# Local attention layers: the output matmuls moved behind the scores, and the turning of queries moved behind the outputs

## The chip, the core and the metric

The kernel runs on one core of one Trainium2 chip, in one launch. The metric is the device time of an execution in microseconds (us); lower is better. The core has five engines that work side by side: PE (TensorE, matrix multiply), DVE (VectorE), ACT (ScalarE), POOL (GpSimd) and SP (SyncE, which only issues DMAs here).

## The reference, cut to what matters

Four batches of 1024 tokens with 128 features pass through two blocks. Block 0 is a linear attention and a routed mixture of experts. Block 1 is a windowed attention with a global prefix, followed by a small network of two *local layers*. The change lies in these local layers alone. One local layer computes, per batch:

```python
h = shift_token(x)                       # half of the features come from the token before
q, k, v = split(h @ wqkv, 3)             # 8 heads of 64
q, k = l2norm(q) * qs, l2norm(k) * ksc   # per head
q, k = rotary_xpos(q, k)
o = local_attention(q, k, v)             # 64-token windows, each sees itself and the one before
x = x + o @ wo
x = x + gated_mlp(layernorm(shift_token(x)))
```

Everything is computed in fp32.

## The kernel before

The local layers are done in 64 tiles of 128 tokens (2 layers x 4 batches x 8 tiles), numbered g = 0 to 63. A tile passes through a software pipeline. One pass of the main loop (L1140 ff., "iteration g") does a different step for each of several tiles:

- `scores` (L949) of tile g: 16 matmuls q·k in 64x64 pieces of the PE array (each fp32 matmul is two PE instructions, so the profile counts 32), then on DVE eight reductions (L968, tile `pr<-s`) which also give the row maximum `mx`.
- `project_mid` / `project` (L652) of tile g+3, once for queries (w=0) and once for keys (w=1): a 128x512 matmul `qk` (L658), its square on ACT (`sq`, L661), two products with the rotary tables on DVE (`co`, L663, and `si`, L668), a sum over the squares on DVE (`ss`, L670), and on POOL the sum co+si (L678) and the norm's power (L674). ACT and DVE read the same PSUM tile `qk`; in the built program the DVE instruction `co` carries a wait on ACT, for `sq`.
- `flip` (L997) of tile g-2, for each half: four PE transposes of the probabilities (`ptr`, L1002), and a copy to SBUF on ACT (`pt`, L1004).
- `over_sums` (L983) of tile g-1: division by the row sums, one half on POOL and one on DVE (L995); for a few early tiles ("light" ones) on ACT (L993).
- `exps` (L974) of tile g: eight exponentials on ACT (`pr<-pr,mx`, L980), each of which needs its reduction of `scores`.
- `turn` (L887) with w=0 of tile g+2: four PE transposes of the finished query rows `co` (`qktr`, L894), and a copy on ACT (`qT`, L901). Keys are turned by DVE and by DMA instead (`turn_keys`, L915; tiles `tk`, `kd`, `kT`).
- `outputs` (L1007) of tile g-3: 32 PE instructions with 64 columns each (`o`, L1016), then a copy on ACT (`os`, L1020).
- `values` (L934) of tile g-1: a 128x512 matmul `v` (L938) and a copy on ACT (`vs`, L940).
- side work, a few steps per iteration: `project_out` (`yp`, L1027), and the MLP of an earlier half batch: `mlp_in` (`in_m`, L1048, bn_stats on DVE), `mlp_out` (`out_m`, L160; `hn`, L161), `mlp_gate` (`gm`, L1062; three Gelu on ACT, `ge`, L1066, with a table load before them and one back to the exponential behind them), `mlp_up` (`a`, L1071; DVE, L1073), `mlp_down` (`ym`, L1079; DVE, L1080).

With half batches of four tiles, the side work repeats every four iterations: one with `mlp_gate`, one with `mlp_up` and `mlp_in`, one with `mlp_down`, one with `mlp_out` and `project_out`. In what follows these are called the gate, the up, the down and the out iteration.

PE's instructions run in the order in which the Python program writes them (`manual_schedule` for PE). The instructions of ACT, DVE, POOL and SP are put in order by a scheduler at build time, which goes by the program order and by its own estimate of when operands are ready; once built, each engine executes its list strictly in that order. Six PSUM tiles of one bank each (pool `p8m`, tag `mid`) are shared in turn by all steps but `scores`, which has two banks of its own.

Of the kernel before, what the change touches and what calls it, by code (L numbers as in the profile page):

```python
# [28 lines left out]
NT = N // P  # L29
# [19 lines left out]
def adaln_blocks(ctx: ExitStack, tc: tile.TileContext, a: dict, out: bass.AP):  # L49
# [637 lines left out]
    EARLY = 3  # L687
# [3 lines left out]
    with (  # L691
# [95 lines left out]
        def project_out(b, k):  # L787
            s = slice(k * BLK, (k + 1) * BLK)
            yp = ps.tile([P, BLK], F32, tag="m", name=f"y1_{b}_{k}")
            pe.matmul(yp, lhsT=wout1, rhs=kept1[b, k, "os"], start=True, stop=True)  # L790
            dve.scalar_tensor_tensor(xT[b][:, s], yp, mods[1][:, 2, b : b + 1], xT[b][:, s], ALU.mult, ALU.add)
# [23 lines left out]
        def when(g, f, *args):  # L815
            if 0 <= g < NG8:
                f(*divmod(g, NT), *args)
# [59 lines left out]
    with (  # L877
# [226 lines left out]
        for l in range(DEPTH):  # L1104
            for b in range(B):
                g = (l * B + b) * NT
# [33 lines left out]
        for g in range(-1, tiles + 4):  # L1140
            side = steps.get(g, [])
            when(g, scores)
            when(g + 3, project_mid, 0)

            turns = {-1: (0, 1), 0: (2,)}.get(g, (g + 2,))
            if 0 < g < NT - 2:
                when(g + 2, turn, 0)
            when(g - 2, flip, 0)
            when(g - 1, over_sums)
            when(g + 3, project_mid, 1)  # L1150
            when(g - 2, flip, 1)
            when(g, exps)
            for i in turns:
                if not 0 < g < NT - 2:
                    when(i, turn, 0)
                if i < EARLY and g < EARLY:
                    when(i, turn, 1)
            when(g - 3, outputs)
            if g > 0:
                when(g + 2, turn_keys)  # L1160
            for f, args in side[:1]:
                f(*args)

            for i in {0: (), 1: (0,)}.get(g, (g - 1,)):
                when(i, values)

            f0 = g - 7
            if f0 % 4 == 0 and 0 <= f0 < tiles - NT:
                lo = f0 % NT * P
                project_out(f0 // (B * NT), f0 // NT % B, lo, lo + BLK)  # L1170
            for f, args in side[1:]:
                f(*args)
# [127 lines left out]
```

## Time and profile before

| | |
|---|---|
| median of 3 runs | 1219.28 us (1216.90 to 1220.04) |
| the profiled execution: its time | 1217.85 us |
| its span in the profile | 1216.0 us, so 1.85 us lie around the span |
| PE busy | 1117.8 us (92%) |
| DVE busy | 893.6 us (73%) |
| ACT busy | 799.8 us (66%) |
| POOL busy | 797.0 us (66%) |
| local layers | from about 573 us to the end |
| busy shares from 840 to 940 us | PE 98.7%, DVE 93.8%, POOL 90.7%, ACT 81.0% |

The busy time of an engine is the time in which the profiler shows an instruction on it. PE's ends are modelled, so that a PE that always has an instruction is not the same as a PE that can't go faster. The chain of waits is the chain of work that ended last, followed back from the last instruction: it tells which engine the end really waited for. A line of the timeline gives the start, the length, the engine, the line of the kernel, the operation and how many were merged; "idle before" is the engine's gap ahead of it, with what ended that gap.

### The profile page before, as it was taken

Reading aid. Unit: us, or ns where it says so; the run is one execution under the profiler, and the core shown is the slowest. Engines: PE = TensorE matmul, PEld = TensorE weight load, DVE = VectorE, ACT = ScalarE, POOL = GpSimd, SP = SyncE. Lnnn points to the kernel's source line nnn. Section 1 sums busy time; section 2 is a strip of 40 time slices with the busy share of each in tenths; the row PEclk is TensorE's granted clock in tenths of the full one; section 3 lists DMA queues with packets and bytes.
Section 4 is the critical chain, followed back from the end, with each engine's and each line's share of the span. In section 5 each row is a group of like instructions: output and inputs, shape, how many; then the busy total and the mean of one; then the engine's idle time right before and its main releaser. Section 6 shows DMA issues by size and latency. Waiting matters only on the chain.

```text
span 1216.0 us, 33934 instructions
## 1 busy us (share of the span) xinstructions
PE 1117.8 (92%) x13142; PEld 677.8 (56%) x13142; DVE 893.6 (73%) x2702; ACT 799.8 (66%) x2189; POOL 797.0 (66%) x712
## 2 busy tenths in 40 slices
PE   6789998999888999978899999999999999999998
PEld 5544453444366666655665555555655556555564
DVE  5557273442475577756989999999999999999854
ACT  3353372232476677755798877878878888788772
POOL 4536454747422062516899999899998999888821
PEclk9799999999999899989999999999999999999999
DMA  6030403022132132210234333343333333333320
GB/s 183 1 125 17 140 1 119 23 66 75 28 91 74 53 101 73 68 44 23 75 114 115 100 101 92 88 111 112 106 93 87 106 109 105 110 94 99 104 59 26
DMA packets 111700, 100.68 MB, mean 83 GB/s; under 512 B 9482, under 2 KB 84788, under 8 KB 111540
## 3 DMA queue, kind: packets, MB, share of 16 engines
q1 hardware_dynamic: 111108, 98.00, 27.9%
q8 instruction: 103, 1.69, 0.6%
q10 hardware_dynamic: 432, 0.53, 0.1%
q14 instruction: 57, 0.47, 0.1%
HBM read 57.71 MB, written 20.86 MB: 65 GB/s over the span
## 4 chain that ended last, share of the span: by engine, by line
PE 43%; DVE 26%; ACT 16%; issue 6%; POOL 6%; DMA 2%; SPq 2%; POOLq 0%; ACTq 0%
PE h L496 5%; DVE pr L968 4%; ACT pr L980 4%; PE ptr L751 3%; PE qk L658 3%; DVE si L668 3%; DVE ss L670 3%; DVE tk L921 2%; DVE co L663 2%; PE yp L1027 2%; PE s L958 2%; PE s L269 2%; PE obank L768 2%; PE y L510 2%; PE gm L1062 2%
## 5 line engine op out<-in xcount | busy, mean ns | idle before, releaser
L980 ACT ACTIVATE pr<-pr,mx 128x128 f32<-128x128 f32 x512 | 200.5, 403 | 51.2 <-DVE mx L968 50.5
L678 POOL TENSOR_TENSOR co<-co,si 128x512 f32<-128x512 f32 x123 | 157.7, 1285 | 68.7 <-DVE si L668 67.4
L674 POOL TENSOR_TENSOR ss<-ss,nhalf 128x16 f32<-128x16 f32 x64 | 194.6, 3041 | 5.2
L968 DVE CUSTOM_DVE_ANT_0 pr<-s,masks,ss 128x128 f32<-128x128 f32 x512 | 144.2, 345 | 12.9 <-PE s L958 12.9
L658 PE MATMUL qk<-wqkv,hs 128*128 128x512 f32 x256 | 140.4, 631 | 4.5 <-ACT pt L753 4.5
L500 POOL TENSOR_TENSOR u<-u,cw 128x512 f32<-128x512 f32 x64 | 82.0, 1283 | 81.7 <-ACT u L498 81.7
L496 PE MATMUL h<-hT,w 128*128 128x512 f32 x256 | 122.9, 603 | 6.0 <-DVE g L502 6.0
L502 DVE TENSOR_TENSOR g<-u,h 128x512 f32<-128x512 f32 x64 | 43.9, 686 | 109.1 <-POOL u L500 109.1
L498 ACT ACTIVATE u<-h 128x512 f32<-128x512 f32 x64 | 38.2, 597 | 123.2 <-PE h L496 113.9
L663 DVE TENSOR_TENSOR co<-qk,ab 128x512 f32<-128x512 f32 x128 | 86.6, 676 | 36.1 <-ACT sq L661 36.1
L290 DVE TENSOR_REDUCE mx<-s 128x8 f32<-128x896 f32 x64 | 66.8, 1086 | 51.8 <-PE s L279 51.8
L661 ACT ACTIVATE sq<-qk 128x512 f32<-128x512 f32 x128 | 75.3, 588 | 44.4 <-PE qk L658 44.1
L980 ACT ACTIVATION_READ_ACCUMULATOR pr<-pr,mx 128x1 f32 x512 | 102.1, 199 | 0.0
L1002 PEld LDWEIGHTS ptr<-ident,pr 128*128 128x128 f32 x512 | 63.4, 141 | 63.4 <-issue 50.9
L995 POOL TENSOR_TENSOR pr<-pr,sm 128x512 f32<-128x512 f32 x64 | 78.7, 1229 | 14.2 <-DVE sm L988 7.9
L668 DVE TENSOR_TENSOR si<-qk,ab 128x512 f32<-128x512 f32 x128 | 87.1, 681 | 0.0
L496 PEld LDWEIGHTS h<-hT,w 128*128 128x128 f32 x256 | 47.7, 193 | 69.9 <-issue 50.5
L670 DVE TENSOR_REDUCE ss<-sq 128x8 f32<-128x512 f32 x128 | 86.4, 675 | 0.0
L958 PEld LDWEIGHTS s<-kT,qT 64*64 64x64 f32 x2048 | 56.4, 134 | 43.6 <-issue 24.3
L958 PE MATMUL s<-kT,qT 64*64 64x128 f32 x2048 | 72.3, 278 | 7.1 <-DMA kT<-kd 6.4
L1002 PE MATMUL ptr<-ident,pr 128*128 128x128 f32 x512 | 76.4, 273 | 0.8 <-POOL pr L995 0.7
L753 ACT COPY pt<-ptr 112x512 f32<-112x512 f32 x128 | 71.6, 612 | 8.1 <-PE ptr L751 8.0
(217 smaller groups left out, 2747.9 us busy)
## 6 DMA issues: line engine op xcount, KB each, us to landing
kT<-kd SPq DMA_DIRECT2D x53, 384.0 KB, 3.5
cw<-cd SPq DMA_DIRECT2D x128, 128.0 KB, 3.0
kd<-tk SPq DMA_DIRECT2D x61, 256.0 KB, 2.4
ve<-vs SPq DMA_DIRECT2D x120, 128.0 KB, 2.3
vb<-dv SPq DMA_DIRECT2D x32, 216.0 KB, 2.8
hs<-hT SPq DMA_DIRECT2D x16, 256.0 KB, 3.8
dv<-vt SPq DMA_DIRECT2D x32, 72.0 KB, 1.6
kT<-kd SPq DMA_DIRECT2D x8, 256.0 KB, 2.7
```

The source lines that it names most:

```text
L496: pe.matmul(hh[:, i], lhsT=w[:, c * P : (c + 1) * P], rhs=hT[b][:, blk(k)], start=True, stop=True)
L500: pool.tensor_tensor(u, u, kept[b, k, "cw"][:, c, :], ALU.mult)
L658: pe.matmul(ps, lhsT=hs[l, b][:, t * P : (t + 1) * P], rhs=wl[l][0][:, w, :], start=True, stop=True)
L663: dve.tensor_tensor(co, ph, abs_[l][:, 0, t, w, :].unsqueeze(1).to_broadcast([P, HEADS, DH]), ALU.mult)
L668: dve.tensor_tensor(si.rearrange("p h (i e) -> p h i e", i=2), ex, sn, ALU.mult)
L670: late["summed"] = dve.tensor_reduce(ss[:, w, :], sq, AX.X, ALU.add)
L674: pool.tensor_tensor(ss, ss, nhalf[:, 0:2].unsqueeze(2).to_broadcast([P, 2, HEADS]), ALU.pow)
L678: pool.tensor_tensor(co, co, si, ALU.add)
L958: pe.matmul(S[j][qs, c, :].rearrange("p (g i) -> p g i", i=32), lhsT=q[rw, c, qs], rhs=k[rw, 2 * e : 2 * e + 4, c, :], start=True, stop=True,)
L968: dve.tensor_tensor_reduce(out=pr[:, c, :], in0=S[j][:, c, :], in1=mk[:, min(t, 1), :], scale=kept[l, b, t, "ss"][:, 0, h : h + 1], scalar ...
L980: act.activation(pr[:, c, :], pr[:, c, :], AF.Exp, bias=mx[:, j, c : c + 1], scale=-1.0, accum_out=sm[:, j, c : c + 1])
L1002: pe.transpose(tp[:, c, :], pr[:, c, :], ident)
```

## The change

In each iteration `outputs` of tile g-3 moves from behind `exps` and the query turns to directly behind `scores` of tile g. `turn(g+2, w=0)` moves to directly behind `outputs`, ahead of the query projection of tile g+3. Before, it stood there or near there only for 0 < g < 6 (behind the query projection), and behind the exponentials of tile g otherwise. For g = -1 and g = 0, which fill the pipeline, the turns of tiles 0, 1 and 2 stay where they were. No instruction is added or removed: each engine has the same operations before and after, in another order.

```diff
             when(g, scores)
+            when(g - 3, outputs)
+            if g > 0:
+                when(g + 2, turn, 0)
             when(g + 3, project_mid, 0)
-
-            turns = {-1: (0, 1), 0: (2,)}.get(g, (g + 2,))
-            if 0 < g < NT - 2:
-                when(g + 2, turn, 0)
             when(g - 2, flip, 0)
             when(g - 1, over_sums)
             when(g + 3, project_mid, 1)
             when(g - 2, flip, 1)
             when(g, exps)
-            for i in turns:
-                if not 0 < g < NT - 2:
-                    when(i, turn, 0)
-                if i < EARLY and g < EARLY:
-                    when(i, turn, 1)
-            when(g - 3, outputs)
+            for i in {-1: (0, 1), 0: (2,)}.get(g, ()):
+                when(i, turn, 0)
+                when(i, turn, 1)
             if g > 0:
                 when(g + 2, turn_keys)
```

## Prediction

> **What bounds the kernel now.** I read the page first. PE is busy 92% of the span and 98.7% between 840 and 940 us, so PE looks like the bound, and the change is about PE's order. But the page's chain of waits gives PE less than half:
>
> ```profile
> PE 43%; DVE 26%; ACT 16%; issue 6%; POOL 6%; DMA 2%; SPq 2%; POOLq 0%; ACTq 0%
> ```
>
> So I asked for the chain of waits between 860 and 910 us alone, the middle of the local layers (start, length, engine, tile, line):
>
> ```profile
> 867.41 0.60 DVE hT L1028
> 868.37 0.88 ACT pr L980 x4
> ...
> 871.55 1.92 ACT pr L980 x10
> 873.48 0.47 ACT qT L901
> 873.95 0.48 ACT os L1020
> ...
> 879.36 0.49 ACT pr L980 x2
> 879.85 0.49 ACT sq L661
> 880.37 0.69 DVE co L663
> ...
> 905.68 0.59 DVE hT L1028
> 906.67 0.88 ACT pr L980 x4
> ```
>
> There is no PE piece in it. The end waits for a loop of two engines that closes once in four iterations: ACT from the first exponential of the gate iteration (868.37) to the first square of the up iteration (880.33), then DVE without a gap through the down and out iterations to the next gate iteration's first reduction (906.22), then ACT again at 906.67. The period is 906.67 - 868.37 = 38.3 us, and the scores of the gate iterations (866.72, 905.06 in the timeline) follow at the same pace. The waits from 828 to 1020 us, five periods, say the same (waiter <- releaser: total, times, longest):
>
> ```profile
> DVE co L663 <- ACT sq L661: 6.2, 5, 1.3
> DVE pr L968 <- PE s L958: 5.9, 5, 1.3
> PE in_m L1048 <- ACT qT L901: 1.2, 5, 0.3
> ```
>
> Once per period DVE stands 1.24 us for the square of the up iteration, and once 1.2 us for its scores; these are DVE's only idle stretches above 0.06 us. PE itself stands 0.3 to 0.4 us per period, for ACT's late query copy. PE is nearly full, but a faster PE alone moves neither end of the loop.
>
> **What PE saves.** PE's timeline of an out iteration (start, length; the difference of two starts is what a group costs):
>
> ```profile
> 857.53 1.12 PE L658 MATMUL qk<-wqkv,hs 128*128 128x512 f32 x2
> 858.50 0.60 PE L1002 MATMUL ptr<-ident,pr 128*128 128x128 f32 x4
> 858.93 1.02 PE L658 MATMUL qk<-wqkv,hs 128*128 128x512 f32 x2
> 859.79 0.60 PE L1002 MATMUL ptr<-ident,pr 128*128 128x128 f32 x4
> 860.23 0.60 PE L894 MATMUL qktr<-ident,co 128*128 128x128 f32 x4
> 860.76 0.34 PE L1016 MATMUL o<-pt,ve 128*64 128x64 f32 x4
> ```
>
> The projection behind the 64x64 scores takes 0.97 us to the next start, the other 0.86: 0.11 for leaving the small tiles. Four transposes cost 0.44, but 0.53 ahead of the 64-column outputs: 0.09 for entering them. Leaving the outputs costs 0.10 more ahead of the next start (0.22 against 0.12 inside the group), and 0.10 inside a 512-wide successor or 0.06 inside transposes. With scores and outputs adjacent, one full-array stretch between them goes, with one entry and one exit. Left are scores to outputs, priced like scores to projection, and outputs to query turn (0.10 + 0.06). Saved: 0.11 + 0.09 + 0.20 - 0.16 = 0.24 us, 0.20 where transposes follow; over the 61 tiles that have both steps about 61 x 0.23 = 14 us of PE time. By the Trainium skill (TensorEngine Tiling (Array Packing), "Tiling Modes") each change of tiling mode drains the array; it names no time, and scores and outputs are two modes, so by it their border is not free either, as I took it. If PE were the bound, rule and rows together would make the sum 14 us faster; by the chain they give nothing in the steady stage.
>
> **What ACT pays.** The built order of the changed program tells it. The two copies `os` and `qT` stood behind the eight exponentials; now they stand where their matmuls end, ahead of the squares. In the gate iteration ACT did two exponentials, square, copy, exponential, square, copy, five exponentials, qT, os, table load, three Gelu, vs, table load. Now: two exponentials, os, qT, exponential, square, copy, exponential, square, copy, four exponentials, table load and so on. The same instructions lie between its first exponential and the first one of the up iteration: 879.36 - 868.37 = 11.0 us both times, if nothing comes late. Nothing should: `os` can start 2.2 us after the scores begin and `qT` 2.8, ACT reaches them at 2.4 and 2.9; the first projection ends at 3.6, and ACT reaches the square at 3.7. These margins of 0.1 us are thin.
>
> In the up iteration, table load, exponential, square becomes table load, exponential, os, qT, square. Both copies are now between the loop's start and the square: 0.48 + 0.47 = 0.95 us later. DVE's `co` can't be drawn ahead of it: it waits on ACT and started at 880.37, 0.04 us behind the square's end. The Trainium skill (PSUM — Partial Sum Buffer, "PSUM bank collisions raise a hardware error") says why such a wait stands: two engines must not read one bank and quadrant at once. It speaks against this change; by it the 0.95 us are due, and without such a wait the steady stage would cost nothing.
>
> DVE also waits in the gate iteration now. Its eight reductions end 1.8 us after ACT's first exponential, the square ends at 0.8 (two exponentials) + 0.95 + 0.39 + 0.57 = 2.7: 0.9 us idle. That is covered by the 1.06 us that DVE stood before the up iteration's scores (875.79) and the 1.26 before its `co`; without that cover it would be 0.9 us more per period. In the down and out iterations os and qT come ahead of the first exponential and fill time in which ACT stood idle (2.22 us from 885.90, 1.95 us from 895.53): no cost, and DVE's stretch from 880.37 to 906.22 stays 25.85 us.
>
> So a period is 38.3 + 0.95 = 39.25 us. Twelve such periods lie between the gate iterations at 671 and 1138 us: **+11.4 us**. Bounds: 0.5 per period (6 us) if DVE makes up a part, 0.95 + 0.9 (22 us) if the second wait is not covered.
>
> **The early tiles.** In iterations 3 to 5 (593 to 620 us) ACT's new order puts the first square behind five exponentials, os and qT, for 4 and 5 behind one or two light divisions as well. From the first reduction: 0.45 + 5 x 0.39 + 0.95 + 0.39 + 0.57 = 4.3 us, while the reductions take 2.2; in iteration 5 DVE stood 0.36 us at that place. That is 1.2 to 2.0 us in each, 3.6 to 6.0; DVE's idle of 0.88, 0.35 and 1.10 us between 608 and 619 us takes some back, and iteration 6 adds under 1. I take **+4 us**, between -1 (PE is on the chain at 593 and 627 to 637 us and saves 0.2 a tile) and +8.
>
> **The rest costs nothing.** The turn now needs POOL's sum of co and si earlier: in the out iteration it ended at 855.44, and the turn starts 2.1 us behind the scores at 856.50, so 3.2 us remain; in the gate iteration 5. The outputs need `pt` copies that end 5 us before. The moved steps issue no DMA; SP's list swaps one `ve` with a `kT`, which is read over 10 us later. The six PSUM tiles rotate in another order: `in_m` now takes the bank of the key projection, about 0.3 us late, PE time off the path. The tail from 1147 us saves 0.2 us for three tiles: 0.
>
> Sum: 1217.85 + 11.4 + 4 = 1233.3 us against the profiled execution; the median was 1.4 us above that one, so I forecast **1234 us**. A measurement can tell about 0.3% (3.7 us) from no change.
>
> **Rivals.** *PE is the bound after all* (faster). For it: 98.7% busy. Then each tile is 0.23 us shorter, 1217.85 - 14 = 1204 us. Against it: no PE piece in the chain, and DVE's 25.85 us stretch has no gap to give. It decides if DVE's wait for the up iteration's square stays at 1.2 us.
> *The copies hide* (no change). ACT is 19% idle; if the 0.95 us were taken from idle time, only the early tiles would count: 1222 us. Against it: ACT's timeline has no gap from 868.37 to 885.9.
> *The second wait adds* (slower still). If DVE's 0.9 us in the gate iteration is not covered, or the thin margins are missed so that os or qT stall ACT, 12 x 0.9 = 11 us more: 1245 us.
>
> **How the numbers follow.** Forecast 0.75, with its own range 1223 to 1242 (6 to 15 steady, -1 to 8 early). PE bound 0.10, hidden 0.05, second wait 0.10. Faster 0.10, same 0.05, slower 0.85. The range 1219 to 1245 leaves out the first rival and about half of the last.
>
> **What would show it.** Right: the distance of the gate iterations' first exponentials grows from 38.3 to about 39.2; DVE's wait on ACT's square in the up iteration grows from 1.24 to about 2.3 and one of 0.9 appears in the gate iteration; scores to outputs costs PE about 0.2 between starts and the projection is 0.86; PE stands idle for other engines, over 1.5 us per period. Wrong: an unchanged or shorter period, PE in the chain of 860 to 910 us, or turns that wait for POOL.

## The result, and the profile after

The changed kernel takes 1231.6 us (median of 4 runs, 1230.19 to 1235.49), against 1218.09 us for the kernel before, measured beside it. The ratio is 1.0125 with a 95% interval of 1.0089 to 1.0161: slower by 13.5 us. The forecast was 1234 us, in a range of 1219 to 1245. The profiled execution took 1230.19 us. One of the ten runs of `up_square_first` below took 1294.72 us at a granted clock of 0.84, where all other runs quoted here had 0.97 to 0.98, and is left out.

The page of the changed kernel first: the span, PE's busy time with its share of the span and its instructions, and the engines' shares in the chain of waits.

```profile
span 1226.6 us, 33918 instructions
PE 1115.1 (91%) x13142; PEld 674.5 (55%) x13142; DVE 892.8 (73%) x2702; ACT 805.2 (66%) x2189; POOL 788.2 (64%) x712
...
DVE 37%; PE 34%; ACT 16%; issue 5%; POOL 4%; DMA 2%; SPq 1%; ACTq 0%; POOLq 0%
```

PE has less to do than before (1115.1 us against 1117.8) and its share in the chain went down, from 43% to 34%; DVE's went up, from 26% to 37%. That points to something other than PE at the end. The chain of waits between 870 and 925 us shows one full period of the loop (start, length, engine, tile, line):

```profile
870.41 0.88 ACT pr L980 x4
871.76 0.49 ACT qT L901
872.63 0.49 ACT sq L661
...
881.41 0.49 ACT pr L980 x2
882.38 0.49 ACT qT L901
882.87 0.51 ACT sq L661
883.40 0.69 DVE co L663
...
908.69 0.60 DVE pr L995
909.66 0.88 ACT pr L980 x4
```

The period is 909.66 - 870.41 = 39.25 us, where it was 38.3. In the up iteration the query copy `qT` (and the output copy `os`; the view shows the longest pieces alone) now stands between the exponential and the square, and DVE's `co` follows the square. DVE's timeline gives the two waits (in brackets: idle before, and who ended it), the first in the gate and the second in the up iteration of the changed kernel:

```profile
873.15 0.69 DVE L663 TENSOR_TENSOR co<-qk,ab 128x512 f32<-128x512 f32 x1 [0.94 <-ACT sq L661]
883.40 0.69 DVE L663 TENSOR_TENSOR co<-qk,ab 128x512 f32<-128x512 f32 x1 [2.55 <-ACT sq L661]
```

Before there was no wait for a square in the gate iteration, and 1.26 us in the up iteration:

```profile
880.37 0.69 DVE L663 TENSOR_TENSOR co<-qk,ab 128x512 f32<-128x512 f32 x1 [1.26 <-ACT sq L661]
```

The waits from 838 to 1034 us, five periods, show who now waits for ACT's copies (waiter <- releaser: total, times, longest):

```profile
DVE co L663 <- ACT sq L661: 17.4, 10, 2.6
PE a L1071 <- ACT os L1020: 5.2, 5, 1.0
```

DVE's wait was 6.2 us in five periods and is 17.4. PE stands about 1 us per period ahead of `a`, for an `os` copy that frees its PSUM tile. From 840 to 940 us PE is busy 95.8%, where it was 98.7%: 1.6 us idle per period.

To say where the 10.6 us between the two spans (1216.0 and 1226.6) lie, I cut each trace at three instructions of DVE's timeline: the first score reduction of tile 0, of tile 12 (a gate iteration) and of tile 60 (the last gate iteration). The stretches between them are called early, steady (twelve periods) and tail in what follows. A period runs from one gate iteration's first score reduction to the next one's; the fourth to the eighth of the twelve are called the middle periods (38.30 to 38.40 us before, 39.23 to 39.27 after, 38.33 and 39.24 on the mean).

| us | until tile 0 | early | steady | tail |
|---|---|---|---|---|
| before | 574.6 | 97.97 | 466.55 | 76.92 |
| after | 571.5 | 101.16 | 475.55 | 78.41 |
| difference | -3.1 | +3.2 | +9.0 | +1.5 |

The first column is code that the change doesn't touch: until 560 us each engine does the same instructions in the same order in both kernels. In the runs below it lies between 572.4 and 575.6 us with no relation to what was edited, so I count its -3.1 us as no effect of the change. The local layers lost 13.7 us.

### The profile page after: what moved, and what is told of

Read it like the earlier page. It is cut to its first block, busy times and chain, and to the rows that moved or that the text cites. A ratio compares the mean times of both kernels' runs of the same rounds, so it can differ in the third digit from the quotient of the medians.

```text
span 1226.6 us, 33918 instructions
## 1 busy us (share of the span) xinstructions
PE 1115.1 (91%) x13142; PEld 674.5 (55%) x13142; DVE 892.8 (73%) x2702; ACT 805.2 (66%) x2189; POOL 788.2 (64%) x712
## 4 chain that ended last, share of the span: by engine, by line
DVE 37%; PE 34%; ACT 16%; issue 5%; POOL 4%; DMA 2%; SPq 1%; ACTq 0%; POOLq 0%
PE h L496 6%; DVE pr L968 5%; DVE ss L670 5%; DVE si L668 4%; DVE tk L921 4%; DVE co L663 4%; PE ptr L751 3%; ACT pr L980 3%; DVE pr L995 3%; PE y L510 2%; PE s L269 2%; ACT sq L661 2%; POOL u L500 2%; PE obank L768 2%; DVE ge L1073 2%
## 5 line engine op out<-in xcount | busy, mean ns | idle before, releaser
L674 POOL TENSOR_TENSOR ss<-ss,nhalf 128x16 f32<-128x16 f32 x64 | 187.1, 2924 | 5.2
L658 PE MATMUL qk<-wqkv,hs 128*128 128x512 f32 x256 | 132.3, 600 | 5.2 <-ACT pt L753 3.7
L995 POOL TENSOR_TENSOR pr<-pr,sm 128x512 f32<-128x512 f32 x64 | 78.2, 1222 | 7.1 <-DVE sm L988 7.1
```

Source lines behind the costliest of these rows:

```text
L658: pe.matmul(ps, lhsT=hs[l, b][:, t * P : (t + 1) * P], rhs=wl[l][0][:, w, :], start=True, stop=True)
L674: pool.tensor_tensor(ss, ss, nhalf[:, 0:2].unsqueeze(2).to_broadcast([P, 2, HEADS]), ALU.pow)
L995: eng.tensor_tensor(pr, pr, bc(sm[:, j, :], [P, 4, P]), ALU.mult)
```

## The experiments

My theory: the loop of ACT and DVE bounds the steady stretch, the two copies ahead of the up iteration's square lengthen it by their 0.95 us, and PE's saving is real but off the path. The first rival: PE bounds the stretch, and the change slows PE in some way that I did not see, for example by waits on PSUM tiles in their new order. The second: the loss comes from the new order as a whole, not from that one place.

**The two copies alone, in the up and in the down iteration.** Both kernels are the kernel before with two added ACT copies of 512 columns that nobody reads, once per period of the steady stretch. Nothing else moves.

```diff
             when(g, scores)
+            if 11 < g < tiles - 3 and g % 4 == 1:      # two_copies_down: == 2
+                with tc.issue_after(kept["vs"].ins):
+                    dm = wp.tile([P, BLK], F32, tag="dm", name=f"dm_{g}", bufs=1)
+                    for i in range(2):
+                        late["dm"] = act.copy(dm, wl[0][0][:, i, :])
...
+            if w == 0 and late.get("dm") is not None:
+                order.enter_context(tc.issue_after(late.pop("dm").ins))
             act.activation(sq, ph, AF.Square)
```

> The kernel before, with two added ACT copies of a 128x512 tile (weights into a scratch tile that nobody reads) ahead of the first square of each up iteration (g = 13, 17, ... 57, twelve of them). PE's order is that of before. If the loop ACT - DVE carries the end (my theory), the square ends 0.95 us later and each later period goes from 38.3 to about 39.2 us: +9 to +12 us in all, about what the change costs, without any move on PE. If PE is the bound, ACT (19% idle in the stage) swallows them: within 2 us of before.

> The kernel before, with the same two added ACT copies, but ahead of the first square of the down iterations (g = 14, 18, ... 58), where ACT stands about 2.2 us idle. My theory: the copies fill that idle time, the period stays 38.3 us, within 2 us of before. If more ACT work costs wherever it stands: as much as in the up iterations, +9 to +12 us.

In the up iteration the copies cost 1234.84 us, ratio 1.0132 (1.009 to 1.0174): the whole loss of the change, with PE's order untouched. The steady stretch is 478.89 us (+12.3), its middle periods 39.35 to 39.40, where they were 38.30 to 38.40. Its waits from 828 to 1025 us:

```profile
DVE co L666 <- ACT sq L664: 11.4, 5, 2.3
```

2.3 us per period instead of 1.26: the copies go into DVE's wait one for one. The same two copies in the down iteration cost nothing: 1217.94 us, ratio 0.9989 (0.9965 to 1.0013), steady stretch 466.54 us. ACT's timeline there shows why:

```profile
885.35 1.30 ACT L1150 COPY dm<-wqkv 128x512 f32<-128x512 f32 x2
887.64 0.60 ACT L664 ACTIVATE sq<-qk 128x512 f32<-128x512 f32 x1 [0.99 <-PE qk L658]
```

Behind the copies ACT still stands 0.99 us for PE. So here the place decides, not the number of instructions: 1 us of ACT work costs 1.0 us per period in one iteration, and nothing in the next.

**Half of the output projection left out.** The same question from PE's side. The kernel is the one before, but only two of the four chunks of `os` are multiplied into each output projection, so that half of its contraction is missing.

```diff
-            for c in range(4):
-                pe.matmul(yp, ..., start=(c == 0), stop=(c == 3))
+            for c in range(2):
+                pe.matmul(yp, ..., start=(c == 0), stop=(c == 1))
```

> The kernel before with two of the four matmuls of each output projection left out in the local layers (half of its contraction; 4 of 8 tiles a group, some 27 us of TensorE in all). Two rivals for what bounded the kernel before. TensorE (98.7 per cent busy in the profile): the time falls by 20 to 27 us, to 1191 to 1198. The loop of ScalarE and VectorE, with TensorE only just behind it: the period of 38.3 us stays within 0.3, and the time falls by 0 to 6 us, 1212 to 1218.

PE's and DVE's timelines of one period:

```profile
861.31 1.88 PE L1027 MATMUL yp<-os,wo 128*128 128x512 f32 x4
...
878.51 0.69 DVE L663 TENSOR_TENSOR co<-qk,ab 128x512 f32<-128x512 f32 x1 [2.58 <-ACT sq L661]
```

The projection has four PE instructions instead of eight, and the scores behind it start 1.81 us later (861.31 to 863.12) where eight take 3.43 us in the changed kernel's chain of waits (at 705.89 us): about 1.6 us less PE time in every period. The middle periods stay at 38.30 to 38.37. DVE gets its scores earlier and waits all the longer for the square: 2.58 us at one place instead of 1.06 + 1.26 at two. That excludes PE as the bound of these periods. The time fell to 1211.81 us, ratio 0.9933 (0.991 to 0.9956), just below the lower end that I had given for this theory (1212). The gain of 6.2 us in the span lies in the tail (-2.8), in three of the twelve periods (the second, the ninth and the eleventh, -0.7 each) and in the early tiles (-0.9). In the tail PE counts: the chain of waits of the kernel before goes through three `yp` there. The three periods can't be put down to PE's time alone, since DVE's list was built otherwise too: in the ninth and the eleventh it has one division (L995) less ahead of the next gate iteration's first reduction.

**Each half of the change alone.** `outputs_only` moves the outputs behind the scores and leaves the turn of queries; `turn_only` moves the turn ahead of the query projection and leaves the outputs.

```diff
 outputs_only
             when(g, scores)
+            when(g - 3, outputs)
...
-            when(g - 3, outputs)
 turn_only
             when(g, scores)
-            when(g + 3, project_mid, 0)
...
-            if 0 < g < NT - 2:
+            if g > 0:
                 when(g + 2, turn, 0)
+            when(g + 3, project_mid, 0)
...                                          # and no turn behind the exponentials for g > 0
```

> Only the outputs are moved behind the scores; the turn of queries stays where it was before. ACT then does os alone ahead of the up iteration's square (table load, exponential, os, square). My theory: half of the 0.95 us per period, 0.48, so 5 to 6 us in the steady stage and 1 to 2 in the early tiles: 1222 to 1226 us. If PE is what counts, this part has nearly the whole gain on PE (scores and outputs are adjacent): faster than before, 1206 to 1210 us.

> Only the turn of queries is moved, directly behind the scores; the outputs stay where they were before. ACT then does qT alone ahead of the up iteration's square. My theory: 0.47 us per period, 5 to 6 us in the steady stage and 1 to 2 in the early tiles: 1222 to 1226 us, and both halves add up to the whole. If PE is what counts: no change, since scores and outputs are as far apart as before.

They take 1225.01 us, ratio 1.004 (1.0012 to 1.0067), and 1223.31 us, ratio 1.0027 (1.0003 to 1.0051). The middle periods are 38.85 and 38.81 us on the mean, where they were 38.33. Each half brings one ACT copy ahead of the square, and they cost 0.52 and 0.48 us per period, about one copy (0.47 to 0.48 us). ACT's way from the gate iteration's first exponential (of tile 32) to the up iteration's `co` says the same: 12.00 us before, 12.49 with either half, 12.99 with both. So no part of the loss needs the two together.

**The change, with the up iteration's copies behind the square.** For tiles 13 to 57 `os` and `qT` are copied behind the first square in the up iteration; PE's order is that of the change.

```diff
+            up = 11 < g < tiles - 3 and g % 4 == 1
+            if not up:
+                copy_out()                    # os and qT, collected by outputs and turn
             when(g + 3, project_mid, 0)
+            if up:
+                copy_out(late["sq", 0])       # issued behind the square
```

> The changed kernel with one difference: in the up iterations from g = 13 on ACT does table load, exponential, square, os, qT instead of table load, exponential, os, qT, square (the remaining exponentials follow). PE's order is that of the changed kernel. My theory: the loop gets its 0.95 us back, the period falls from 39.25 to about 38.3 us, 9 to 10 us faster than the changed kernel, so 1221 to 1223 us; what remains against before is the early tiles (about 3 us). If PE's order itself costs the time (banks, waits behind the turn), nothing changes: about 1231 us.

> The same kernel as up_square_first, for a profile at full clock: the first timing gave 1.0055 of before. My theory: a steady period of about 38.3 us, with what remains of the loss in the early tiles (about 3 us) and in the last stretch behind the gate iteration of tile 60 (about 2 us). If the steady period is well above 38.3 us, another wait has taken the place of the one removed.

The time is 1224.92 us (median of nine runs), ratio 1.0055 (1.0033 to 1.0076); the profile is of another execution of the same kernel, 1224.56 us. So half of the loss came back, less than I had expected. The middle periods are 38.53 to 38.56, not 38.3: 0.69 of the 0.91 us came back. ACT's way to the first `co` is 12.01 us again, as before. What is left lies behind it: `os` and `qT` now stand ahead of the up iteration's second square, and DVE's second `co` starts 1.95 us behind the first (883.17 to 885.12), 0.03 us behind the end of that square, where it was 1.79 (880.37 to 882.16). DVE's wait in the gate iteration is still 0.94 us; it lies within ACT's way and adds nothing to it. The rest of the loss lies where this edit does not reach, in the early tiles (100.88) and the tail (79.49).

**The squares ahead of everything.** If that square bounds the loop, it can be made earlier than it was before the change. In the up iteration ACT had: three Gelu, `vs`, table load, one exponential, square. `squares_only` has PE's order of the kernel before and only this ACT order turned, in the up iterations 13 to 57: Gelu, square, `vs`, `pt`, second square, `pt`, `qT`, `os`, table load, eight exponentials. The squares and copies need no table load, so the load moves behind them. `squares_ahead` has the same idea (the copies `os` and `qT` between the squares) with PE's order of the change for tiles 8 to 60.

```diff
 squares_only
+            up = 12 < g < tiles - 3 and g % 4 == 1
             when(g + 3, project_mid, 0)
+            if up:
+                for f in late_values:                      # the vs copy
+                    with tc.issue_after(late["sq", 0].ins):
+                        f()
...
-            when(g, exps)
+            if not up:
+                when(g, exps)
             ...
                 when(g - 3, outputs)
+                copy_out()
+                if up:
+                    when(g, exps)
 squares_ahead, against squares_only
-            early = 64 <= g < 0          # with early: outputs and turn directly behind scores
+            early = 8 <= g < 61
...
+                copy_out(late["sq", 0])
```

> The changed order on PE for g = 8 to 60, the order of before for the first eight and the last iterations; and in the up iterations ACT does the first square directly behind the Gelus, then vs, os and qT, the second square, and only then the table load and all eight exponentials. My theory: the way from the gate iteration's first exponential to the up iteration's square loses a table load (1.28), an exponential (0.39) and vs (0.58), the loop could close in about 37 us, and now PE's own time, 0.9 us per period less than before, sets the period: 37.4 to 37.8 us. That is 0.5 to 0.9 us for each of twelve periods, 6 to 10 us faster than before, 1208 to 1212 us. If the loop does not explain the loss, the time stays near 1231 or, if only the early tiles mattered, near 1219 us.

> The kernel before with its PE order unchanged, and only ACT's order in the up iterations turned: Gelus, first square, vs, copy, second square, copy, qT, os, then table load and eight exponentials. It takes the loop ACT - DVE away as the bound without the change. My theory: PE becomes the bound with the order of before, 38.3 us less the 0.35 us that it waited: a period of 37.9 us, 3 to 6 us faster than before (1212 to 1215 us), against 1203 us with the changed order: the difference, 0.9 us or a little more per period, is then what the moved outputs and turns save on PE. If PE's order is worth nothing: 1203 us here too. If the turned ACT order is worth nothing by itself: 1218 us.

Both are faster than either kernel: `squares_ahead` takes 1203.17 us, ratio 0.987 (0.9829 to 0.9911), and `squares_only` 1204.12 us, ratio 0.9871 (0.9831 to 0.9911). For both I had expected a smaller gain: the middle periods fell not to 37.4 or more but to 36.75 to 36.85 us, and not to 37.9 but to 37.54. What bounds them now is PE. The chain of waits of `squares_only`, one up iteration (start, length, engine, tile, line):

```profile
869.16 1.03 PE s L975 x32
870.20 1.05 PE qk L658 x2
...
872.99 0.44 PE qktr L904 x4
873.43 1.08 PE o L1037 x32
874.51 2.77 PE a L1092 x6
```

And that of `squares_ahead`:

```profile
868.75 1.03 PE s L975 x32
869.79 1.08 PE o L1037 x32
870.87 0.59 PE qktr L904 x4
871.46 0.86 PE qk L658 x2
...
873.61 0.52 PE ptr L1023 x4
874.14 2.68 PE a L1092 x6
```

From 860 to 905 us both chains have PE pieces alone, and every piece starts where the last one ends. Here, where PE is on the path, the change's saving can be read and counts. The first projection takes 0.86 instead of 1.05, and 512-wide groups are shorter where no outputs stand ahead of them (2.77 here, 2.58 for `gm` at 865.32 in the same chain of `squares_ahead`), against 0.15 more for the turn. In the up iteration shown, 0.08 is lost at the second `ptr` and 0.10 at `a`. The middle periods are 36.75 to 36.85 instead of 37.54: 0.77 us per period, 0.19 a tile.

That `squares_ahead` is no faster in sum has its reason at the edges: early stretch 100.09 and tail 78.58 us, where `squares_only` has 98.07 and 76.16. In both kernels the steady stretch, 449.15 and 453.90 us, is far below the 466.55 of before. In the time itself the new order on PE does not show: 1203.17 and 1204.12 us is what I had named for an order that is worth nothing. That it pays per period rests on the traces.

**Where the early tiles lose.** `early_only` has the change for g < 8 and the order of before from 8 on. `squares_ahead_later_start` is `squares_ahead` with PE's new order from 12 on instead of 8.

```diff
 early_only, against the changed kernel
-            when(g - 3, outputs)
-            if g > 0:
+            early = 0 < g < 8
+            if early:
+                when(g - 3, outputs)
                 when(g + 2, turn, 0)
...
+            if not early:
+                ...                          # turn and outputs where they were before
 squares_ahead_later_start, against squares_ahead
-            early = 8 <= g < 61
+            early = 12 <= g < 61
```

> The change for iterations below 8 alone, the order of before from 8 on. The prediction put the early tiles at +4 us, the comparison of the two profiles at +3.2 (the stretch up to tile 12's first score reduction 97.97 to 101.16 us). If it is those early iterations: early stretch 101, steady 466.5, tail 77, time 1221 to 1222. Rival: what the early stretch gains or loses goes with the time at which the local layers are reached (571.5 us after, 574.6 before) or with iterations 8 to 12, where the order is old here: stretch 98, time 1218.

> The changed order on TensorE from iteration 12 only (squares_ahead: from 8); ScalarE's order of the up iterations as in squares_ahead. If the 2.0 us that squares_ahead lost before tile 12's first score reduction (100.09 us where the kernel before has 97.97) came from the early iterations 8 to 11, where ScalarE's order was not turned, they come back: early stretch 98 us, steady 449 to 450, tail 78.5, time 1200.5 to 1202. Rival: the 2.0 us are a matter of when the local layers are reached, not of the order in iterations 8 to 11; then the early stretch stays at 100 and the time at 1203.

The early stretch is 100.25 us with the change in tiles below 8 (1222.05 us, ratio 1.0023, 1.0001 to 1.0045), 100.09 with it from 8 on, 97.94 with it from 12 on (1202.27 us, ratio 0.9858, 0.982 to 0.9896), and 101.16 with it in all. Six profiles of kernels with the old order up to tile 11 and all the work have 97.94 to 98.17. So the loss of 3.2 us is due to the order, and lies in tiles 1 to 7 and in 8 to 11 alike, 2.2 and 2.1 us if each is done alone; they don't add up fully. Of the two halves of the change, `outputs_only` has 99.63 us there and `turn_only` 98.29, so the turn alone costs little there, and the outputs alone about half of the loss. The time of `squares_ahead_later_start` can't be told from that of `squares_ahead`, nor from that of `squares_only`.

**The squares first in the gate iterations too.** The last experiment asks if the loop still has a hand in the new period.

```diff
+            gate = 11 < g < tiles - 3 and g % 4 == 0
-            if not up:
+            if not up and not gate:
                 copy_out()
             when(g + 3, project_mid, 0)
+            if gate:
+                copy_out(late["sq", 0])
```

> squares_ahead_later_start, and ScalarE does in the gate iterations too the first square ahead of the output and query copies (behind three of the eight exponentials). VectorE's wait of 0.93 us in the gate iteration goes to 0 to 0.3. My theory, that TensorE bounds the loop once the squares are ahead: the steady stretch stays at 449 to 450 us (periods 36.8), and only the tail may gain, by 1 to 2 us where gate iteration 60 loses its wait: 1199 to 1202. Rival, the loop of ScalarE and VectorE still sets the period: periods fall by up to 0.9 to 35.9, and the time to 1190.

It took 1205.08 us, ratio 0.9875 (0.9836 to 0.9914), above the 1199 to 1202 that I had expected, but not to be told from its base. The wait in the gate iteration is gone, but no gain comes of it: the middle periods are 36.97 to 37.17, a little longer than 36.8, and the steady stretch 451.71. PE is alone in the chain from 860 to 905 us here too, so there was nothing to get from ACT. In the up iteration ACT itself now stands for PE:

```profile
870.50 0.60 ACT L661 ACTIVATE sq<-qk 128x512 f32<-128x512 f32 x1 [0.52 <-PE qk L658]
```

## Why the prediction was right, point by point

**The bound.** It was the loop of ACT and DVE, not PE. Two runs show it from both sides: 1 us more ACT work at one place in the loop gave 12.3 / 12 = 1.03 us per period, and 1.6 us less PE work gave 0 in the middle periods. The rival that PE is the bound, with its chance of 0.10, fell; it read a busy share of 98.7% as a limit.

**What ACT pays.** The period went from 38.3 to 39.24 us, with 39.25 forecast. The other signs stood as announced: a wait of 0.94 us in the gate iteration (0.9 forecast), no stall of ACT at the thin margins of 0.1 us there, PE idle 1.6 us per period (over 1.5). The wait in the up iteration was 2.55 us, 0.25 more than the 2.3 forecast; the wait of 1.06 us for scores went in exchange. The cover for the second wait held, and the rival of 1245 us fell; so did that of hidden copies (1222 us). The turn did not wait for POOL: its first transpose starts 0.15 us behind the start of the last output instruction in every tile between 800 and 1000 us.

**The PSUM rule.** In the up iteration shown, `co` started 0.03 us behind the end of the square's record (882.76 + 0.61 us to 883.40), and each copy put ahead of the square moved it by a copy's length (ACT's way to `co` is 12.00, 12.49 and 12.99 us with none, one and two). That agrees with the Trainium skill's rule (PSUM — Partial Sum Buffer, "PSUM bank collisions raise a hardware error") by which these two reads are kept apart; the runs show the wait, not what would happen without it.

**The size of the steady stretch.** Forecast were 12 x 0.95 = 11.4 us, measured +9.0. The term that was mis-sized is the count of twelve equal periods. The last ten lost 1.0 us each on the mean (0.87 to 1.14), but the first changed by -1.2 and the second by +0.2.

The order of ACT's list shows why the copies cost nothing there. From the third period on, two copies (`os` or `qT`) stand between the gate iteration's first exponential and the up iteration's `co` before, and four after; that way is 0.99 us longer each time. In the first two periods there are two in both kernels, because after the change the gate iteration's own copies come ahead of its first exponential: in iteration 16 `os` starts at 711.49 us, `qT` at 712.07, the exponential at 713.32, and the way from there takes 12.68 us before and 12.67 after. In `two_copies_up`, where the added copies stand inside this way in all twelve periods, the first two lost 0.9 and 1.1 us like the others.

The -1.2 us are DVE's. From the up iteration's `co` on (686.33 us before, 686.36 after) it works with no idle stretch above 0.04 us up to the first reduction of tile 16. Before, a division stands on its list ahead of that reduction:

```profile
712.78 0.18 DVE L988 RECIPROCAL sm<-sm 128x8 f32<-128x8 f32 x1
713.00 0.99 DVE L995 TENSOR_TENSOR pr<-pr,sm 128x512 f32<-128x512 f32 x1
713.91 0.34 DVE L968 CUSTOM_DVE_ANT_0 pr<-s,masks,ss 128x128 f32<-128x128 f32 x1
```

After, that reduction comes first:

```profile
712.25 0.71 DVE L1028 TENSOR_TENSOR hT<-hT,yp 128x512 f32<-128x512 f32 x1
712.81 0.41 DVE L968 CUSTOM_DVE_ANT_0 pr<-s,masks,ss 128x128 f32<-128x128 f32 x1
```

So 27.57 us became 26.45; `less_output_projection`, with PE's order of before, has the same list there and 26.43. PE is on the changed kernel's chain of waits from 689.5 to 714.6 us, but no run shows that its saving shortened this period, and why the scheduler placed the division elsewhere is open.

The lists of the two built programs could have told me: I counted ACT's instructions in one period and multiplied. The period list of the kernel before was a warning too, with 41.37 and 38.98 us at its start. That 1234 us came within 2.4 us of the measured time is partly luck: the steady stretch was put 2.4 us too high, the early tiles 0.8, and the tail 1.5 too low.

**The early tiles.** Forecast +4, measured +3.2, and by the experiments a matter of the order. But I had put it in iterations 3 to 6 alone; about half of it lies in 8 to 11.

**The tail.** Forecast 0, measured +1.5 us, by a single profile each. Kernels with the old order in the tail show 76.2 to 78.5, the two with the whole new order there 78.4 and 79.5, so that a difference of 1.5 lies within what kernels of one order differ by. A wait of 0.94 us in gate iteration 60 with no up iteration's idle to cover it would account for a part; that is argued and not shown.

**PE's saving.** Forecast 0.20 to 0.24 us a tile, measured 0.19 where PE is the bound. The pieces are the ones named: 1.05 to 0.86 for the projection, 2.77 to 2.58 for a 512-wide group behind, 0.44 to 0.59 for the turn. In the kernel as changed, this saving was lost in waits for ACT.

## What to carry to other kernels

An engine that is busy 98.7% of a stretch is not its bound until the chain of waits goes through it. Find the loop in which two in-order queues release each other, list the instructions between its two ends, and count every instruction that a change puts there at full price; one iteration further the same instruction can be free. Then look at the same place for what could leave: here two squares were drawn ahead of a table load and eight exponentials on ACT, which took the bound from the loop, gained 1.3%, and only then made the reordering of PE worth 0.77 us per period in the traces. Before a per-period price is multiplied, check that all the periods are alike, by the order of the instructions in each.

## What the runs showed of the hardware

Scores and outputs use the PE array in pieces of different shape, 64x64 and 128x64. The Trainium skill (TensorEngine Tiling (Array Packing), "Tiling Modes") says that a change of mode drains the array, and gives no time. In the changed kernel the first output instruction starts 199 ns behind the start of the last score instruction (median of 20 tiles between 800 and 1000 us), where two neighbouring score instructions start at most 140 ns apart; in the kernel before, the first projection instruction started the same 199 ns behind it. So the border between the two small modes is not free, and in this distance costs as much as that to the full array. What the reordering spares lies behind the border: the two instructions of the first projection stand 533 ns apart behind the scores and 432 elsewhere, and transposes to outputs took 202 ns where transposes stand 109 apart.

I had not expected that half of the output projection could be taken from PE in every period, in a stretch where it shows almost no idle time, with no effect on the period: 38.30 to 38.40 us with it, 38.30 to 38.37 without it.
